# Last image of a convolution-attention layer: which engine takes the outer taps, and where a range check branches

## The chip, the cores and the metric

The kernel runs on one core of a Trainium2 chip. The core has TensorE (PE, with its weight loads shown as PEld), VectorE (DVE), ScalarE (ACT), GpSimd (POOL), and SyncE (SP), which issues most of the DMAs. The metric is the device time of one execution in microseconds. A profile is one execution of the program on the chip, seen by the hardware profiler; its span runs from the first to the last instruction that it recorded.

## The reference

Eight images of 256 channels and 32 x 32 pixels go through two layers. Layer 0 is a convolutional attention block followed by a gated feed-forward block; layer 1 is attention over tokens with a mixture of eight experts. The change touches the feed-forward block of layer 0 and the point where layer 1 begins. Of layer 0, this part counts:

```python
def _edffn(x, pi_w, dw_w, fft_p, po_w):
    x = _conv1x1(x, pi_w)                 # 256 -> 1024 channels
    x = _dwconv3(x, dw_w)                 # 3 x 3 taps, each channel by itself
    x1, x2 = (x[:, :hid], x[:, hid:])
    x = jax.nn.gelu(x1, approximate=False) * x2
    x = _conv1x1(x, po_w)                 # 512 -> 256 channels
    ...
    xf = jnp.fft.rfft2(xp) * fft_p        # on 8 x 8 patches
    xp = jnp.fft.irfft2(xf, s=(PS, PS))
    ...

a = _attention(_ln(x, norm1_w, norm1_b), ...)
x = x + gamma1 * a
f = _edffn(_ln(x, norm2_w, norm2_b), pi_w, dw_w, fft_p, po_w)
return x + gamma2 * f
```

## The kernel before

All of it is float32. A tile has 128 partitions, which hold 128 channels, and in the free dimension the 1024 pixels of an image or half of them (512). The 1024 hidden channels of the feed-forward block are thus eight groups, n = 0 to 7; group n in the first four (x1) is passed through a Gelu and multiplied with group n + 4 (conv).

**Order.** Most instructions are written through a small class (`InOrder`, whose call is line 72, so that nearly every row of the profile has L72). It ties each instruction to the one that was written before it on the same engine. The order on an engine is therefore the order in which the Python generators are stepped: `together(main, side, ratio)` steps `side` as long as its summed costs lag behind those of `main`. Instructions written as `nc.sync`, `nc.vector` and so on are placed by the scheduler.

**A group.** `open_group(b, n, pad)` (L927) makes the 1x1 convolution of one group on PE, half an image at a time (ph, from a pool of two PSUM banks that nearly all of layer 0's small results share). ACT copies each half into a tile with a border of zeros (`pad`: hpad or vpad), and writes the same half, multiplied by the weight of the middle tap, into the group's result. `tap` (L611) then adds one outer tap on DVE: a scalar_tensor_tensor over 128 x 1024 which reads the pad and the result and writes the result. There are eight outer taps, `OTHERS`. `complete` (L1019) follows the last tap: for the last image it issues the Gelu on ACT at once; then `gate` (L1027) multiplies a finished pair on DVE (two halves) and `mix` (L1050) puts the product through the output convolution on PE. `spectrum` (L1065) follows all groups: a copy on ACT (zf), two small transforms on PE (pf, py) with a product on DVE between them (gf), and DVE's sum into the image (t<-py), at whose end the image is stored (td).

**The last image.** For images 0 to 6 the groups run beside the attention of the next image. Image 7 has nothing beside it but the end of image 6's spectrum and the small `scores_matrix` (L1178), which prepares a matrix for layer 1 in a tile called lin; see L1200 to L1204. There `hidden` is given `on_pe=(2,)`: groups 0, 1 and 3 to 7 are convolved on DVE, one opened ahead of the one that runs, and group 2 by `group_on_pe` (L941), which has PE add all nine taps by matmuls with diagonal matrices (taps, pc).

**Range check and branch.** The attention of layer 0 takes exponentials without subtracting a maximum. Their sums and the reciprocals of these are kept in `accs`; after `spectrum(B - 1)` they are compared with a limit, a matmul counts the partitions where all is well (votes), and DVE writes `bad` (L1215). At L1218 every engine loads `bad` from SBUF and branches: only if it is set, `layer0_shifted` computes layer 0 again with a subtracted maximum. What stands inside and behind the branch is scheduled by itself.

**Behind it.** Constants are loaded (vec2, wrs, brs), then from L1365 layer 1 begins: `load_t` (L1374) loads image 0 as layer 0 stored it, `at` and `wv` are weights, and `first_norm(0)` (L1468) transposes image 0 on PE (tpt), copies it on ACT (zt), takes statistics on DVE (st, mv), a root on POOL, scales on DVE and transposes back (tpz). Nothing runs beside this first norm. Its tiles take the SBUF addresses which layer 0's tiles had.

Of the kernel before, what the change touches and what calls it, by code (L numbers as in the profile page):

```python
# [17 lines left out]
P = 128  # L18
# [6 lines left out]
NE = 8  # L25
# [79 lines left out]
def conv_attn_hybrid_kernel(  # L105
# [371 lines left out]
    with ExitStack() as l0:  # L477
# [137 lines left out]
        OTHERS = (0, 1, 2, 3, 5, 6, 7, 8)  # L615

# [324 lines left out]
        def group_on_pe(b, n):  # L941


            assert ready2[b]
            diag = one.tile([P, 9, P], F32, tag="xn", name="taps")
            pad = vpad[n % 2]
            for h in range(2):
                hs = slice(h * HALF, (h + 1) * HALF)
                ph = ps_m.tile([P, HALF], F32, tag="mm", name="ph")
                conv1x1(ph, piw, n * P, xn2[b], hs)  # L950
                act.activation(interior(pad, h), rows(ph), AF.Identity, bias=pi_o[:, n : n + 1])
            for k in range(9):
                act.activation(diag[:, k, :], ident, AF.Copy, scale=dw_w[:, n, k : k + 1])
            yield
            dst = group_tile(n)
            r = H // 2
            for h in range(2):
                pc = ps_m.tile([P, HALF], F32, tag="mm", name="pc")
                for k in range(9):
                    r0 = h * r + k // 3  # L960
                    pe.matmul(pc, diag[:, k, :], inside(pad, r0, k % 3, r), start=(k == 0), stop=(k == 8))
                act.copy(dst[:, h * HALF : (h + 1) * HALF], pc)
                if h == 1:
                    hid_of[b]["h"][n] = dst
                    complete(b)
                yield

        def hidden(b, lead, on_pe=(), alone=False):
# [3 lines left out]
            on_dve = [n for n in range(2 * ng) if n not in on_pe]  # L972
# [19 lines left out]
            hid = hid_of[b] = {"h": {}, "out": [], "gelu": 0, "alone": alone}  # L992
            others = [(g, 3 * i) for i, g in enumerate(on_pe)]
            beside = {}
            for g, at in others:

                beside[at, 6], beside[at + 1, 6], beside[at + 2, 1] = g, g, g
            running = {}
            for m, n in enumerate(on_dve):
                pad, dst = cur  # L1000
                for i, k in enumerate(OTHERS):
                    if m + 1 < len(on_dve):
                        if i == 3:
                            opening = open_group(b, on_dve[m + 1], hpad[(m + 1) % 2])
                            cur = next(opening)
                            next(opening)
                        if i == 5:
                            next(opening)
                    if (m, i) in beside:
                        g = beside[m, i]  # L1010
                        if g not in running:
                            running[g] = group_on_pe(b, g)
                        next(running[g])
                    tap(dst, pad, dw_w[:, n, :], k)
                    yield 1.3
                hid["h"][n] = dst
                complete(b)
# [186 lines left out]
        together(rest(), hidden(B - 1, (), (2,), alone=True), 1.0)  # L1204
# [12 lines left out]

    with tc.If(nc.values_load(bad[0:1, 0:1]) > 0):  # L1218
        layer0_shifted()

    z_d = [dram.tile([P, 2, 3, KC, HALF], F32, tag=f"zd{b}", name=f"zd{b}") for b in range(B)]
    u_d = [dram.tile([P, KC, N], F32, tag=f"ud{b}", name=f"ud{b}") for b in range(B)]
    wm = ctx.enter_context(tc.tile_pool(name="wm", bufs=1))
    more.append(wm.tile([P, NVEC - NVEC0], F32, name="vec2"))  # L1230
    nc.sync.dma_start(more[0], vecs[:, NVEC0:])
    wrs = wm.tile([P, KC, NE], F32, name="wrs")
    nc.sync.dma_start(wrs, wr.rearrange("(k p) e -> p k e", p=P))
    brs = wm.tile([1, NE], F32, name="brs")
    nc.sync.dma_start(brs, br)
    wT = wm.tile([4 * NE, N], F32R, name="wT")
    feats = [wm.tile([P, KC, HALF], F32, name="feat0"), None]
    z2_last = wm.tile([P, KC, HALF], F32, name="z2_last")
    mhalf1 = wm.tile([P, NT], F32, name="mhalf1")
    nc.gpsimd.memset(mhalf1, -0.5)  # L1240

    NG, SLOTS = 2, NE // 2
    w_d = [[dram.tile([P, 3, KC, C], F32, tag=f"wd{e}_{l}", name=f"wd{e}_{l}") for l in range(3)] for e in range(NE)]
    w_in = {}

    def in_parts(e, l):

        return l != 1 or e % 2 == 1

    def load_expert(pool_, e, l):  # L1250

        tag = f"w{e % SLOTS}_{l}"
        if not in_parts(e, l):
            w_ = pool_.tile([P, KC, C], F32, tag=tag, name=tag, bufs=1)
            nc.sync.dma_start(w_, w2[e].rearrange("(k p) o -> p k o", p=P))
        else:
            w_ = pool_.tile([P, 3, KC, C], F32R, tag=tag, name=tag, bufs=1)
            nc.sync.dma_start(w_.bitcast(F32), w_d[e][l])
        w_in[e, l] = w_

    def stacked(dst, src, order):

        first = [order.index(i) for i in range(2)]
        dve.tensor_copy(dst[:, :, first[0]].bitcast(F32R), src)
        dve.tensor_sub(dst[:, :, first[1]].bitcast(F32R), src, dst[:, :, first[0]])
        for i, part in enumerate(order):
            if i not in first:
                dve.tensor_copy(dst[:, :, i], dst[:, :, first[part]])

    def upper(dst, src, eng=None, positive=False):  # L1270

        if eng is None:
            act.activation(dst[:, 0], src, AF.Relu if positive else AF.Copy, scale=DOWN)
        else:
            eng.tensor_scalar_mul(dst[:, 0], src, DOWN)

    def lower_part(dst, src, positive=False):
        high = dst[:, 0].bitcast(F32)
        if positive:
            dve.scalar_tensor_tensor(dst[:, 1], src, 0.0, high, ALU.max, ALU.subtract)  # L1280
        else:
            dve.tensor_sub(dst[:, 1], src, high)

    def difference(dst):
        dve.scalar_tensor_tensor(dst[:, 2], dst[:, 1].bitcast(F32), -STEP, dst[:, 0].bitcast(F32), ALU.mult, ALU.add)

    def layer_norm(src, dst, zt, room, bank):

        n = src.shape[2] // P
        mv = room([P, NT, 2], "mv", 2)  # L1290
        for i0 in range(0, n, 2):
            tp = bank([P, 2, C], "tpt")
            for i in range(2):
                for k in range(KC):
                    c0 = (i0 + i) * P
                    pe.transpose(tp[:, i, k * P : (k + 1) * P], src[:, k, c0 : c0 + P], ident)
            act.copy(zt[:, i0 : i0 + 2, :], tp)
            yield 0.6
            for i in range(i0, i0 + 2):
                st = room([P, 6], "st", 4)  # L1300
                dve.bn_stats(st, zt[:, i, :])
                dve.bn_aggr(mv[:, i, :], st)
            yield 0.6

        y = room([P, NT], "y1", 2)[:, :n]
        r = room([P, NT], "r1", 2)[:, :n]
        pool.tensor_scalar(y, mv[:, :n, 1], LN_EPS, None, ALU.add)
        pool.tensor_tensor(r, y, mhalf1[:, :n], ALU.pow)
        pool.tensor_mul(y, y, r)
        pool.tensor_mul(y, y, r)  # L1310
        pool.tensor_scalar(y, y, -0.5, 1.5, ALU.mult, ALU.add)
        pool.tensor_mul(r, r, y)

        for _ in range(4):
            yield 1.0

        def scaled(i0):
            for i in range(i0, i0 + 2):
                dve.tensor_scalar(zt[:, i, :], zt[:, i, :], mv[:, i, 0:1], r[:, i : i + 1], ALU.subtract, ALU.mult)

        scaled(0)
        yield 1.0
        scaled(2)
        yield 1.0
        for i0 in range(0, n, 2):
            if i0 + 4 < n:
                scaled(i0 + 4)
            tp = bank([P, KC, 2, P], "tpz")
            for i in range(2):
                for k in range(KC):  # L1330
                    pe.transpose(tp[:, k, i, :], zt[:, i0 + i, k * P : (k + 1) * P], ident)
            act.copy(dst[:, :, i0 * P : (i0 + 2) * P], tp.rearrange("p k i c -> p k (i c)"))
            yield 0.9

    def gate(h, room, bank):

        nt = NT // 2
        lg = bank([P, nt, NE], "lg")
        for i in range(nt):
            c0 = i * P  # L1340
# [24 lines left out]
    with ExitStack() as l1:  # L1365
# [45 lines left out]
        def expert_parts():  # L1411

            for e in range(NE):
                for l, src in enumerate((w1, w2, wo)):
                    if not in_parts(e, l):
                        continue
# [230 lines left out]

# [329 lines left out]
```

## Time and profile before

| | us |
|---|---|
| median of 3 runs (lowest, highest) | 3183.1 (3177.9, 3192.1) |
| the profiled execution | 3183.65 |
| its span | 3181.8 |
| busy PE, PEld | 2935.8, 1938.8 |
| busy DVE | 2390.2 |
| busy ACT | 1565.1 |
| busy POOL | 341.0 |
| last image: first tap to last gate | 1322.7 to 1409.3 |
| its spectrum and the check | 1409.3 to 1424.5 |
| from the check to the first matmul of layer 1 | 1424.5 to 1439.4 |
| last instruction that stores the output is issued | 3178.05 |

Busy times are sums over the whole span and say little of a stage of 100 us; what bounds a stretch is read from the stretch alone. In the page's lines "x8" is the number of instructions, and what stands in square brackets is the idle time of the engine before the line and the instruction that ended it. "issue" there means that the profile shows nothing that the engine waited for.

### The profile page before, as it was taken

The page shows a single profiled execution, that of the slowest core. Times are in us where ns is not written, and L with a number is a line of the kernel's source. Part 1 is how long each engine was busy: PE and PEld are TensorE (multiplying, and loading weights), DVE is VectorE, ACT ScalarE, POOL GpSimd, SP SyncE. Part 2 cuts the span into 40 slices and gives each one's busy share as a digit, 9 for nine tenths or more (in the row PEclk, how much of TensorE's full clock was granted, in tenths as well). Part 3 has the DMA queues.
Part 4 walks back from the last instruction along what each step waited for, and adds up shares of the span by engine and source line. Part 5 has one row for each costly group of instructions (what it writes and reads, how often), then busy time and mean ns, then how long its engine had stood idle before and what let it go on. Part 6 is the DMA issues. An engine that isn't in the chain of part 4 may idle for free.

```text
span 3181.8 us, 41598 instructions
## 1 busy us (share of the span) xinstructions
PE 2935.8 (92%) x16802; PEld 1938.8 (61%) x16802; DVE 2390.2 (75%) x3014; ACT 1565.1 (49%) x2312; POOL 341.0 (11%) x419
## 2 busy tenths in 40 slices
PE   5998899899898989868999999999999999999998
PEld 3654555555555555434666666677777777777776
DVE  1378877878787869664767665588988888888887
ACT  1554445555454536313333333365666666666665
POOL 1021211111111110001222222100000000000000
PEclk9998999999999999988999999999999999999999
DMA  5113030212112020002333221422112142211220
GB/s 152 55 27 80 27 80 27 72 36 62 46 47 61 28 66 8 17 14 101 125 131 132 106 103 54 176 76 78 69 67 82 64 172 86 99 67 66 93 73 27
DMA packets 63854, 234.85 MB, mean 74 GB/s; under 512 B 5590, under 2 KB 13862, under 8 KB 54822
## 3 DMA queue, kind: packets, MB, share of 16 engines
q1 hardware_dynamic: 63654, 232.12, 21.9%
q8 instruction: 134, 2.20, 0.3%
q14 instruction: 66, 0.54, 0.1%
HBM read 140.61 MB, written 91.49 MB: 73 GB/s over the span
## 4 chain that ended last, share of the span: by engine, by line
PE 49%; DVE 4%; ACT 1%; issue 0%; POOL 0%; SPq 0%; DMA 0%; ACTq 0%; DVEq 0%
PE pm L72 12%; PE pa L72 11%; PE q L72 11%; PE s L72 4%; PE po L72 4%; PE pv L72 2%; PE pk L72 2%; DVE zt L72 1%; DVE nm L72 1%; PE tp L72 1%; DVE pr L72 1%; PE tpz L72 1%; PE tpt L72 1%; DVE st L72 1%; ACT pr L72 1%
## 5 line engine op out<-in xcount | busy, mean ns | idle before, releaser
L72 PE MATMUL pa<-ze,w 128*128 128x512 f32 x1488 | 423.2, 393 | 0.0
L72 DVE SCALAR_TENSOR_TENSOR x<-hpad,vec,x 128x1024 f32<-128x1024 f32 x248 | 317.0, 1282 | 40.5 <-ACT x L72 33.5
L72 DVE SCALAR_TENSOR_TENSOR conv<-hpad,vec,conv 128x1024 f32<-128x1024 f32 x256 | 329.3, 1293 | 13.9 <-ACT conv L72 7.3
L72 PEld LDWEIGHTS pa<-ze,w 128*128 128x128 f32 x1488 | 278.2, 188 | 63.3 <-issue 3.1
L72 ACT ACTIVATE h<-pa,bn_o,s1a 128x512 f32<-128x512 f32 x256 | 198.7, 776 | 203.4 <-PE pa L72 203.4
L72 ACT ACTIVATE pT<-s 128x1024 f32<-128x1024 f32 x256 | 247.3, 1024 | 71.9 <-PE s L72 71.9
L72 PE MATMUL po<-pT,vT 128*32 128x256 f32 x4096 | 274.0, 385 | 0.0
L72 PE MATMUL q<-h2p,w 128*128 128x512 f32 x768 | 269.0, 459 | 0.0
L72 DVE SCALAR_TENSOR_TENSOR h<-pa,s1b,h 128x512 f32<-128x512 f32 x256 | 191.2, 747 | 93.9 <-PE pa L72 87.8
L72 PE MATMUL ph<-xn,piw 128*128 128x512 f32 x512 | 244.7, 615 | 3.1 <-DVE xn L72 1.6
L72 PE MATMUL pm<-h,w 128*128 128x512 f32 x512 | 240.8, 593 | 0.0
L72 PE MATMUL s<-kk,z 128*128 128x512 f32 x512 | 236.8, 594 | 4.1 <-DVE pr L72 4.1
L72 PE MATMUL q<-z_first,w 128*128 128x512 f32 x768 | 217.2, 391 | 2.7 <-DVE z_first L72 1.7
L72 PE MATMUL pm<-h1p,w 128*128 128x512 f32 x768 | 216.7, 390 | 0.5 <-DVE h1p L72 0.5
L72 DVE SCALAR_TENSOR_TENSOR o<-vpad,pe_w,o 128x1024 f32<-128x1024 f32 x128 | 163.5, 1282 | 45.5 <-ACT o L72 42.3
L72 PEld LDWEIGHTS q<-h2p,w 128*128 128x128 f32 x768 | 144.6, 188 | 83.1 <-issue 59.6
L72 PE MATMUL s<-qst,kst 128*128 128x256 f32 x1024 | 176.1, 314 | 14.5 <-DMA kst<-part 13.2
L72 ACT ACTIVATE hpad<-ph,pi_o 128x512 f32<-128x512 f32 x126 | 86.9, 689 | 182.9 <-PE ph L72 176.0
L72 PEld LDWEIGHTS po<-pT,vT 128*32 128x32 f32 x4096 | 120.8, 110 | 85.9 <-issue 4.2
L72 PEld LDWEIGHTS s<-qst,kst 128*128 128x128 f32 x1024 | 137.5, 193 | 47.8 <-issue 42.9
L72 PEld LDWEIGHTS q<-z_first,w 128*128 128x128 f32 x768 | 144.4, 188 | 34.4 <-DVE z_first L72 2.9
L72 PEld LDWEIGHTS pm<-h1p,w 128*128 128x128 f32 x768 | 144.7, 188 | 31.7 <-DVE h1p L72 0.9
(268 smaller groups left out, 5068.1 us busy)
## 6 DMA issues: line engine op xcount, KB each, us to landing
ze<-zd SPq DMA_DIRECT2D x29, 1536.0 KB, 6.4
qst<-part SPq DMA_DIRECT2D x32, 512.0 KB, 8.7
kst<-part SPq DMA_DIRECT2D x32, 512.0 KB, 14.9
te<-ud SPq DMA_DIRECT2D x32, 512.0 KB, 4.1
wd<-parts_w SPq DMA_DIRECT2D x20, 768.0 KB, 3.7
w<-wd SPq DMA_DIRECT2D x20, 768.0 KB, 4.6
zd<-parts SPq DMA_DIRECT2D x14, 1024.0 KB, 3.8
t<-in_x_dram SPq DMA_DIRECT2D x8, 1024.0 KB, 5.0
```

Of the source, the lines that this page charges most:

```text
L72: return self._tc.keep_in_program_order(method(*args, **kwargs))
```

## The change

It has two parts.

For the last image, `hidden` and `group_on_pe` are replaced by a new function. All eight groups have their taps on DVE, but of group n the first `ON_POOL[n]` outer taps are taken by two other engines: ACT multiplies the shifted image by the tap's weight into a tile (part; four buffers), and POOL adds this to the group's result. Groups are opened two ahead, with four pads (vpad as well as hpad):

```diff
+        ON_POOL = (0, 3, 3, 3, 4, 3, 3, 3)
...
+        def hidden_last(b):
+
+            pads = [hpad[0], hpad[1], vpad[0], vpad[1]]
+            dsts = {}
+            hid = hid_of[b] = {"h": {}, "out": [], "gelu": 0, "alone": True}
+
+            def open_(n):
+                opening = open_group(b, n, pads[n % 4])
+                pad, dsts[n] = next(opening)
+                next(opening)
+                yield 0.0
+                next(opening)
+                for k in OTHERS[: ON_POOL[n]]:
+                    part = two.tile([P, N], F32, tag="pT", name="part", bufs=4)
+                    act.activation(rows(part), inside(pad, k // 3, k % 3, H), AF.Copy, scale=dw_w[:, n, k : k + 1])
+                    pool.tensor_add(dsts[n], dsts[n], part)
+                yield 0.0
+
+            for n in range(2):
+                for _ in open_(n):
+                    pass
+            for n in range(2 * ng):
+                opening = open_(n + 2) if n + 2 < 2 * ng else None
+                for i, k in enumerate(OTHERS[ON_POOL[n] :]):
+                    if opening and i in (0, 2):
+                        next(opening)
+                    tap(dsts[n], pads[n % 4], dw_w[:, n, :], k)
+                    yield 1.3
+                hid["h"][n] = dsts[n]
+                complete(b)
...
-        together(rest(), hidden(B - 1, (), (2,), alone=True), 1.0)
+        together(rest(), hidden_last(B - 1), 1.0)
```

The second part takes the branch from between the layers. All that follows it becomes a function, `tokens`, which is called once without a branch, and a second time inside the branch, at the end of the program, behind `layer0_shifted`. The memory pools of layer 1 are made with `reuse_waits="tile"`, as those of the experts were before, and three of its first loads go to POOL's queue, in order with POOL's other instructions:

```diff
-    with tc.If(nc.values_load(bad[0:1, 0:1]) > 0):
-        layer0_shifted()
...
+    def tokens(stack):
+
+        wm = stack.enter_context(tc.tile_pool(name="wm", bufs=1, reuse_waits="tile"))
...
-        two = l1.enter_context(tc.tile_pool(name="two1", bufs=2))
+            two = l1.enter_context(tc.tile_pool(name="two1", bufs=2, reuse_waits="tile"))
...
-        load_t(0)
+            load_t(0, pool)
             at = wpool.tile([P, KC, C], F32, name="at")
-            nc.sync.dma_start(at, at_d)
+            pool.dma_start(at, at_d)
...
+            wv_s = wpool.tile([P, KC, C], F32, name="wv")
+            pool.dma_start(wv_s, wvT.rearrange("(k p) o -> p k o", p=P))
...
+    with ExitStack() as stack:
+        tokens(stack)
+    with tc.If(nc.values_load(bad[0:1, 0:1]) > 0):
+        layer0_shifted()
+        with ExitStack() as stack:
+            tokens(stack)
```

The rest of the diff is the indentation of what is now inside `tokens`, and the arguments of `hidden` that nothing uses any more.

## Prediction

> **What bounds it now.** I read the page's slices first, then busy time by stretch, then the timelines of DVE and POOL, and last the instructions of the branch. The change lies between 1290 and 1450 us, and at the program's end. The stretches (us, then busy PE, PEld, DVE, ACT, POOL, then TensorE clock and DMA):
>
> ```profile
> 1322.70:1362.10 39.40, 35.89 (x88) 16.26 (x89) 31.36 (x27) 17.86 (x32) 0.00 (x0) 0.96 0.08 34
> 1362.10:1409.30 47.20, 24.52 (x70) 15.46 (x70) 45.99 (x40) 8.80 (x13) 0.00 (x0) 0.81 0.00 0
> 1409.30:1424.50 15.20, 14.08 (x58) 9.71 (x56) 6.28 (x14) 2.24 (x4) 0.00 (x0) 0.82 0.00 1
> 1424.50:1439.40 14.90, 0.00 (x0) 0.02 (x1) 3.02 (x20) 1.79 (x3) 4.62 (x7) 0.64 0.52 182
> ```
>
> In the hidden stage of the last image (1322.7 to 1409.3) DVE sets the end and POOL does nothing; then comes a latency chain, the spectrum, of 15.2 us; then 14.9 us without one matmul, the branch. DVE's timeline in that stage:
>
> ```profile
> 1322.68 1.28 DVE L72 SCALAR_TENSOR_TENSOR x<-hpad,vec,x 128x1024 f32<-128x1024 f32 x1 [4.11 <-ACT x L72]
> 1324.67 30.08 DVE L72 SCALAR_TENSOR_TENSOR x<-hpad,vec,x 128x1024 f32<-128x1024 f32 x23
> 1362.07 10.53 DVE L72 SCALAR_TENSOR_TENSOR conv<-hpad,vec,conv 128x1024 f32<-128x1024 f32 x8 [7.32 <-ACT conv L72]
> 1372.64 1.29 DVE L72 TENSOR_TENSOR hid<-x,conv 128x512 f32<-128x512 f32 x2
> 1373.85 10.52 DVE L72 SCALAR_TENSOR_TENSOR conv<-hpad,vec,conv 128x1024 f32<-128x1024 f32 x8
> ```
>
> Eight taps take 10.52, so a tap costs 1.315 in a row. The 86.6 us are 56 taps (73.6), four gates of 1.21 (4.8), 0.9 for the previous image, and 7.3 idle while PE convolves group 2. Now two places where POOL and DVE read SBUF at once, first in layer 1, then taps beside two POOL copies of half a tile:
>
> ```profile
> 2013.00 2.87 DVE L72 TENSOR_TENSOR parts<-z,parts 128x1024 f32<-128x1024 f32 x1 [1.40 <-ACT parts L72]
> 2012.43 5.64 POOL L72 TENSOR_TENSOR feat<-feat,z 128x1024 f32<-128x1024 f32 x2
> L72 POOL TENSOR_TENSOR feat<-feat,z x12: 2349/2362/3331, 1641.0 to 2014.7; 128x1024 f32<-128x1024 f32 x12
> 791.68 4.38 DVE L72 SCALAR_TENSOR_TENSOR conv<-hpad,vec,conv 128x1024 f32<-128x1024 f32 x3
> 792.30 2.68 POOL L72 COPY vpad<-vfull 128x512 f32<-128x512 f32 x2 [15.95 <-ACT vfull L72]
> ```
>
> The third line gives min/median/max in ns. The DVE operation of 1.22 (a like addition, feat<-feat,scratch, takes 1215 ns) needs 2.87 beside an add and ends only 1.1 us after that add; the second POOL add needs 3.33 instead of 2.35 and ends at 2018.07, 2.20 after DVE's end at 2015.87. They take turns. The boundary and the end:
>
> ```profile
> 1424.40 0.14 DVE L1215 TENSOR_SCALAR bad<-votes 1x1 int32<-1x1 f32 x1
> 1439.41 3.29 PE L72 MATMUL tpt<-ident,t 128*128 128x128 f32 x16 [15.48 <-DMA at<-at_d]
> 1441.27 0.43 DVE L72 BATCH_NORM_STATS2 st<-zt 128x6 f32<-128x256 f32 x1 [2.84 <-ACT zt L72]
> L1218 SPq COMPARE_BRANCH  x1: 50/50/50, 1425.5 to 1425.5; - x1
> L1218 SPq EVENT_SEMAPHORE  x8: 17/17/17, 1426.0 to 1430.1; - x8
> L1218 DVEq COMPARE_BRANCH  x1: 72/72/72, 1425.2 to 1425.2; - x1
> L1218 DVEq EVENT_SEMAPHORE  x1: 21/21/21, 1431.5 to 1431.5; - x1
> 3178.05 0.37 SPq L1808 DMA_DIRECT2D out_dram<-te  x1
> ```
>
> DVE resumes 6.2 us after its branch, ACT and POOL likewise; SP, which jumps over few instructions, after 0.4. Then the loads of layer 1 are issued, and the first statistics come at 1441.27, 16.8 us after the last t<-py (1424.48).
>
> [...]
>
> **The change, part by part.** *Taps.* ON_POOL sums to 22, so DVE keeps 64-22 = 42 taps: 42 x 1.315 = 55.2, with gates 4.8 and the 0.9. PE's group (18 matmuls, nine ACT taps) and DVE's 7.3 idle go. ACT gets 22 products of about 1.05 (as x<-x) and one more opening: some 7 us per group against DVE's 12 to 13, so it keeps ahead; four pads and four part buffers let it. POOL gets 22 adds of 128x1024. *Price of an add on DVE:* one tap and one add in turn take 2.20 + 1.1 + 0.07 (a tap is that much longer than the 1.22) = 3.35, less the tap's 1.315: 2.03. From below, a half-size, one-input copy cost the taps 0.23 (4.38 against 3.92, for two); four times the reads make 0.92. From above, the whole 2.35. I take 2.03: 22 x 2.03 = 44.7 (20 to 52). Nothing hides it: all adds come while DVE has taps queued. *Opening two ahead:* the first step of the generator now opens groups 0, 1 and half of 2 before tap 0. PE's last py of image 6 then stands behind ph of groups 1 and 2, each half waiting for a PSUM bank that ACT frees (1.46 per half): py at about 1326.5 instead of 1321.1, and t<-py is behind tap 0 on DVE, in order, with all further taps behind it: idle 1324.0 to 1327.2, +3.2. Sum 55.2+4.8+0.9+44.7+3.2 = 108.8 against 86.6: **+22.2**.
>
> *Branch gone from the boundary.* t(0), at and wv go to POOL's queue, which is in order behind the adds; by tile sizes t(0) falls on lin, free after about 1335, so it lands long before layer 0 ends. The first transposes then follow the last py on PE, zt's copy takes 0.59, and the first statistics come some 1.3 after the last t<-py, not 16.8: **-15.5**. If the loads wait, bound 8 to 10. What is late next is the chain of the first norm itself (1441.3 to 1449.4), unchanged. The small work that lay in the gap (DVE 3.0, ACT's table load 1.8, POOL's 4.6) loses its cover; the spectrum's idle DVE time can take it, 0 to 4, I take **+1**.
>
> *Branch at the end.* SP is last: store issued until 3178.43, load of bad 0.5, branch 0.1, and now it jumps over the whole second copy of layer 1 as well, so I give it the far target's 6.2, then 0.6 of semaphores, 0.6 of final waits and 0.8 of barrier: 3187.2 instead of 3181.8, as the store's landing (3180.9) is covered. **+5.5** (3 if SP's target comes quickly, 7 at most).
>
> Sum: 22.2 - 15.5 + 1 + 5.5 = +13.2 on the profiled execution's 3183.65 (span 3181.8 and 1.85 around it), which is 0.5 above the median of 3183.1: **3197**. A difference under 0.5% (15.9 us) can't be told from none with this kernel.
>
> **Rivals.** (1) The adds hide beside the taps. For it: POOL is empty, and ACT and PE have room. Against: the 2.87. At no cost for adds the stage is 64.1, -22.5, in all -31.5: 3152. At the lower price, 0.92, it is -11: 3172. (2) The slower side: the boundary still holds layer 1's loads until layer 0's last tiles are free, or the POOL queue issues t(0) only then. From a landing later than the last t<-py it costs; with 5.2 us from issue to landing (1434.07 to 1439.27) the first statistics come 7 after, the gain is 9.8, and the time 3203. For it: one POOL queue, adds first. Against: the addresses, and that the last group's adds are issued two groups early. (3) The branch isn't dear at the end: 3 instead of 5.5 gives 3194; it only shifts the forecast.
>
> **Numbers.** Forecast with (3) 0.67, own range 3187 to 3207, of which about two thirds lie below 3199; rival (2) 0.17; rival (1) 0.16. Faster 0.15 (nearly all of (1)), same 0.46, slower 0.39. The range, 3175 to 3211, takes in the cheaper adds and the dearer ones, and leaves out most of (1).
>
> **What would show it.** Right: POOL busy some 60 us between 1322 and 1432, its adds at 3.3 instead of 2.35, taps beside them spaced 3.3; the last gate near 1431; tpt within 1 us of the last py; SP's last semaphores near the end of the span 6 us after its branch. Wrong: taps at 1.3 beside running adds, DVE waiting for part, a gap before tpt, or ACT ending the waits of the taps.

## The result, and the profile after

The changed kernel takes 3192.7 us (median of 15 runs, 3188.5 to 3196.3) where the kernel before takes 3182.9 (15 runs): a ratio of 1.0029, with a 95% interval of 1.0021 to 1.0037. It is slower by about 10 us, 0.3%. The profiled execution has a span of 3191.4 us against 3181.8.

Cut at the same events in both traces, the span splits so (us, each from the start of the instruction named):

| stretch | before | after | difference |
|---|---|---|---|
| span's start to the last image's first tap | 1322.68 | 1323.08 | +0.4 |
| first tap to the end of the last gate | 86.62 | 108.72 | **+22.1** |
| last gate to the end of the last t<-py (spectrum) | 15.18 | 14.02 | -1.2 |
| last t<-py to layer 1's first statistic (boundary) | 16.79 | 1.92 | **-14.9** |
| first statistic to the issue of the last store | 1736.78 | 1737.41 | +0.6 |
| that issue to the span's end | 3.75 | 6.27 | **+2.5** |
| span | 3181.80 | 3191.42 | +9.6 |

Busy time by stretch of the changed kernel, in the columns used before (us, busy PE, PEld, DVE, ACT, POOL, clock, DMA share, GB/s): first half and second half of the hidden stage, spectrum, and what was the gap at the branch.

```profile
1323.10:1362.70 39.60, 22.75 (x58) 10.63 (x58) 35.84 (x17) 25.16 (x32) 27.53 (x9) 0.80 0.10 36
1362.70:1431.80 69.10, 27.62 (x70) 16.44 (x69) 68.11 (x36) 21.43 (x26) 48.78 (x23) 0.67 0.06 23
1431.80:1445.82 14.02, 12.92 (x57) 8.90 (x56) 6.25 (x14) 4.04 (x7) 1.03 (x1) 0.88 0.00 0
1445.82:1449.00 3.18, 1.94 (x16) 1.73 (x16) 3.08 (x25) 2.05 (x4) 0.00 (x0) 1.00 0.84 273
```

POOL, idle there before, is now busy for 76.3 us of the two halves, and DVE is busy for 103.95 of 108.7 us though it has fourteen taps fewer. A DVE instruction counts as busy also while something holds it up: the twelve taps in the third row below fill 28.73 us, 2.39 each, where a tap in a row takes 1.315. The rows below show DVE's taps and POOL's adds, each from its own timeline (start, duration in us, and in brackets the idle time ahead).

```profile
1323.08 1.28 DVE L72 SCALAR_TENSOR_TENSOR x<-hpad,vec,x 128x1024 f32<-128x1024 f32 x1 [4.11 <-ACT x L72]
1327.73 0.87 DVE L72 SCALAR_TENSOR_TENSOR t<-py,vec,t 128x256 f32<-128x256 f32 x2 [3.37 <-PE py L72]
1328.53 28.73 DVE L72 SCALAR_TENSOR_TENSOR x<-hpad,vec,x 128x1024 f32<-128x1024 f32 x12
...
1444.05 1.77 DVE L72 SCALAR_TENSOR_TENSOR t<-py,vec,t 128x256 f32<-128x256 f32 x4 [0.64 <-PE py L72]
...
1447.74 0.42 DVE L72 BATCH_NORM_STATS2 st<-zt 128x6 f32<-128x256 f32 x1
```

```profile
1327.60 18.80 POOL L72 TENSOR_TENSOR x<-x,part 128x1024 f32<-128x1024 f32 x6 [21.34 <-ACT part L72]
...
1422.34 0.81 POOL L72 DMA_DIRECT2D t<-td  x1 [0.27 <-issue]
...
1425.47 3.92 POOL L1387 TENSOR_SCALAR_AFFINE_SELECT sel<-sel 32x1024 f32<-32x1024 f32 x2
```

From 1327.60 on, POOL runs six adds without a pause, 18.80 us or 3.13 each; DVE's twelve taps in 28.73 include stretches with and without an add beside them. There is no bracket on the DVE row: nothing made it wait by a semaphore. The time is inside the instructions. The view of the adds as a group, by tile, with min/median/max in ns:

```profile
L72 POOL TENSOR_TENSOR conv<-conv,part x13: 2673/3203/3433, 1362.7 to 1418.1; 128x1024 f32<-128x1024 f32 x13
...
L72 POOL TENSOR_TENSOR x<-x,part x9: 2360/3210/3322, 1327.6 to 1359.5; 128x1024 f32<-128x1024 f32 x9
```

The add that starts at 1327.60, while DVE is idle, takes 2.36. The median is 3.2: beside taps an add is stretched as well, by some 0.85 us. At the boundary PE has the first transpose 0.1 us after the last t<-py (1445.82), and the loads that had been behind the branch were issued by POOL's queue at 1422.34 already (t<-td, 5.9 us to landing), ahead of the spectrum:

```profile
1445.92 1.94 PE L72 MATMUL tpt<-ident,t 128*128 128x128 f32 x16 [0.66 <-DVE bad L1208]
```

At the end of the program, the branch (instructions of line 1849 in the tile view's columns: duration min/median/max in ns, first and last start):

```profile
L1849 SPq EVENT_SEMAPHORE  x8: 17/17/17, 3189.3 to 3189.8; - x8
...
L1849 POOLq COMPARE_BRANCH  x1: 45/45/45, 2130.5 to 2130.5; - x1
...
L1849 PEldq COMPARE_BRANCH  x1: 3835/3835/3835, 3182.2 to 3182.2; - x1
...
L1849 SPq COMPARE_BRANCH  x1: 50/50/50, 3186.1 to 3186.1; - x1
```

SP resumes 3.1 us after its branch (3186.1 + 0.05 to 3189.3). In the kernel before, where only the second computation of layer 0 stands inside the branch, it needed 0.4. But the others, which needed 5.7 to 6.3 there, now take 2.8 to 3.8. POOL, which has no work after 2130, branches at 2130.5 already.

### The profile page after: what moved, and what is told of

Read it like the earlier page. It is cut to its first block, busy times and chain, and to the rows that moved or that the text cites. A ratio compares the mean times of both kernels' runs of the same rounds, so it can differ in the third digit from the quotient of the medians.

```text
span 3191.4 us, 41548 instructions
## 1 busy us (share of the span) xinstructions
PE 2922.1 (92%) x16766; PEld 1931.6 (61%) x16766; DVE 2415.3 (76%) x3000; ACT 1585.3 (50%) x2325; POOL 416.5 (13%) x444
## 4 chain that ended last, share of the span: by engine, by line
PE 76%; DVE 15%; ACT 3%; POOL 2%; DMA 2%; issue 2%; SPq 0%; ACTq 0%; DVEq 0%; POOLq 0%
PE pm L72 12%; PE pa L72 11%; PE q L72 11%; PE po L72 10%; PE s L72 8%; PE ph L72 6%; DVE conv L72 3%; DVE x L72 3%; PE pq L72 3%; PE sums L72 3%; DVE o L72 2%; PE pz L72 2%; PE pv L72 2%; PE pk L72 2%; DVE hid L72 1%
## 5 line engine op out<-in xcount | busy, mean ns | idle before, releaser
L72 DVE SCALAR_TENSOR_TENSOR conv<-hpad,vec,conv 128x1024 f32<-128x1024 f32 x233 | 303.8, 1311 | 5.8
L72 PE MATMUL ph<-xn,piw 128*128 128x512 f32 x512 | 251.3, 628 | 28.5 <-ACT conv L72 12.9
L72 PEld LDWEIGHTS ph<-xn,piw 128*128 128x128 f32 x512 | 94.4, 198 | 139.9 <-issue 95.4
L72 PE MATMUL pz<-pow__116,hid 128*128 128x256 f32 x512 | 136.1, 421 | 34.6 <-DVE hid L72 34.6
## 6 DMA issues: line engine op xcount, KB each, us to landing
kst<-part SPq DMA_DIRECT2D x32, 512.0 KB, 14.9
```

Of the source, the lines that this page charges most:

```text
L72: return self._tc.keep_in_program_order(method(*args, **kwargs))
```

## The experiments

All times are medians; each ratio is against runs of the kernel before on the same chip in the same session. "Stage" is first tap to last gate, "boundary" and "end" are cut as in the table above.

| kernel | us | ratio, 95% interval | stage | boundary | end |
|---|---|---|---|---|---|
| branch alone moved | 3169.9 | 0.9971 (0.9961, 0.9981) | 88.3 | 1.9 | 6.6 |
| taps alone moved | 3201.1 | 1.0059 (1.0046, 1.0072) | 107.2 | 16.7 | 3.7 |
| no taps for POOL | 3176.9 | 0.9986 (0.9978, 0.9995) | 94.5 | 1.9 | 6.7 |
| add of part to itself | 3180.1 | 0.9994 (0.9985, 1.0002) | 98.8 | 1.9 | 6.4 |
| add of another tile | 3193.8 | 1.0032 (1.0021, 1.0042) | 108.9 | 1.9 | 6.4 |
| fill instead of add | 3150.5 | 0.9896 (0.9881, 0.9911) | 65.5 | 1.9 | 6.3 |
| copy instead of add | 3163.7 | 0.9937 (0.9922, 0.9952) | 80.7 | 1.9 | 6.7 |
| no branch at all | 3188.3 | 1.0017 (1.0010, 1.0024) | 108.8 | 1.9 | 3.9 |
| transfer at the branch | 3191.4 | 1.0023 (1.0014, 1.0031) | 108.7 | 1.9 | 6.5 |
| last image stored early | 3183.1 | 0.9997 (0.9989, 1.0006) | 86.6 | 14.4 | 3.7 |
| two ahead, one group on PE | 3163.3 | 0.9943 (0.9929, 0.9956) | 81.0 | 1.9 | 6.8 |
| two ahead, two groups on PE | 3158.9 | 0.9919 (0.9905, 0.9932) | 73.0 | 1.9 | 7.0 |

### The two parts by themselves

The changed kernel with the hidden stage of before, and the kernel before with the new hidden stage:

```diff
 # branch alone moved: in the changed kernel
-        together(rest(), hidden_last(B - 1), 1.0)
+        together(rest(), hidden(B - 1, (), (2,), alone=True), 1.0)
 # taps alone moved: in the kernel before
-        together(rest(), hidden(B - 1, (), (2,), alone=True), 1.0)
+        together(rest(), hidden_last(B - 1), 1.0)
```

> Only the second part: layer 1 follows without a branch, the branch stands at the program's end, and image 7 is convolved as before (group 2 on PE, no POOL adds). Theory (the lock: POOL's adds and DVE's taps exclude each other, and the parts simply add up): the two traces give -14.9 us at the boundary, +2.5 at the end and about -0.5 between, so about 3170, with the last gate of layer 0 where it was before (1409). Rival (the boundary gained only because the new stage left PE, ACT or the SP queue early): well under 10 us gained, 3174 or more.

> Only the first part: the taps of image 7 by ACT and POOL, groups two ahead, none on PE; the branch stays between the layers. Lock theory: the hidden stage is 22 us longer, so about 3205, and the sum of this and of the branch-only kernel is the whole change. Rival (the stage is long because layer 1's early loads and constants are mixed into it): less than 15 us longer, under 3198.

Measured: 3169.9 and 3201.1, that is -12 and +19 us by the medians; the ratios say -9 (between -12 and -6) and +19 (between +15 and +23). Together this is +7 to +10, which agrees with the +10 of the whole change. So the change is a gain of 9 to 12 from the branch and a larger loss from the taps, and the stretches lie where the table above has them (boundary 1.92, stage 107.2). The stage with the taps alone grew by 20.6, where 22 was expected, and the kernel came to 3201 and not 3205. With the branch alone the stage is 1.7 longer than before: POOL's constants for layer 1, which used to be made in the gap, now run beside the taps (a gate of 2.20 us instead of 1.29, a row of eight taps of 11.35 instead of 10.52). With the taps alone moved they are still made in the gap, and the stage is 1.5 shorter than in the changed kernel.

### Is it POOL's part, or the new order of the groups?

```diff
-        ON_POOL = (0, 3, 3, 3, 4, 3, 3, 3)
+        ON_POOL = (0, 0, 0, 0, 0, 0, 0, 0)
```

> The changed kernel with ON_POOL all zero: every outer tap on DVE, POOL adds nothing, groups still opened two ahead and none on PE. Lock theory: 64 taps of 1.315 make 84.2, with gates 4.8, 0.9 and the wait of 3.4 93 us in place of the 108.7 with POOL's help, so about 15 us faster than the changed kernel: 3177. Rival (adds cost DVE little, the stage is long for its order or for ACT): 22 more taps of 1.315, 29 us slower: 3221.

All 64 outer taps on DVE, and 3176.9: 16 us faster than with POOL's help, 14.2 of them in the stage itself. So it is POOL's part. A tap given to ACT and POOL costs DVE more than a tap kept: 14.2 / 22 = 0.65 us more.

### What is the price of an add: waiting for its result, or the memory?

Four kernels leave everything in place and change what POOL does with the partial product. In all four no tap and no gate uses what POOL computes, and 22 of the last image's 64 outer taps are left out of the result.

```diff
-                    pool.tensor_add(dsts[n], dsts[n], part)
+                    pool.tensor_add(part, part, part)               # add of part to itself
+                    pool.tensor_add(part, part, xn2[b][:, 0, :])    # add of another tile
+                    pool.memset(part, 0.0)                          # fill
+                    pool.tensor_copy(part, part)                    # copy
```

> The changed kernel, but POOL adds each part to itself and not to the group's result, so that no tap waits for an add: 22 of the 64 outer taps are left out of the result. Same engines, same shapes, two SBUF inputs. Lock theory: within 2 us of the changed kernel, 3191 to 3195, taps beside an add still 3.3 us apart. Rival (DVE waits for POOL's results at the start of each group): the stage shrinks to 64 to 70 us, about 3150.

Measured: 3180.1, which fits neither. The rival (the taps waited for POOL's results) is far off at 3150, but the cost was a quarter less than the theory had it. The trace showed why the experiment was not clean: an add of a tile to itself is a shorter instruction, 1.89 us where it runs alone. So it was repeated with two different tiles, and with instructions that read one tile and none:

> The 22 adds of POOL now add another tile of the same size to the partial product and leave the sum in the partial product; nobody waits for it, and 22 of the last image's 64 outer taps are left out of the result. An add of two different tiles should take 2.36 us where it runs alone, as in the changed kernel. If what an add costs VectorE is the time in which it holds it from the memory (2.03 us each in the changed kernel), the stage stays at 107 to 109 us and the kernel at 3191 to 3195. If the cost was that taps or gates waited for the adds to arrive, the wait is gone here and the stage is 42 x 1.315 + 6 + 3 = 64 us: 3150 (no more than 3155). 3180, what adding a tile to itself gave, would mean that its shorter duration was not the reason for that result.

> POOL's 22 adds are replaced by 22 copies of the partial product onto itself (one input; 22 of the last image's 64 outer taps are left out of the result). If the price of a POOL instruction to VectorE is its own duration less 0.3 us whatever it reads, a copy of about 0.9 to 1.0 us costs 0.6 to 0.7 each and the stage is 77 to 80 us: 3162 to 3165. If only instructions with two inputs hold VectorE off, the stage is 64 to 66 us: 3147 to 3151.

> POOL's 22 adds are replaced by 22 fills of the same tile with zero (no input is read; 22 of the last image's 64 outer taps are left out of the result). If only POOL's reads of two tiles hold VectorE off, the taps keep 1.31 us each, the stage is 64 to 66 us and the kernel 3147 to 3151. If every POOL instruction on a tile of this size alternates with the taps, by its own duration less 0.3 us, a fill of 0.5 to 1 us costs 0.2 to 0.7 each: 3152 to 3163.

All three times came out where the theory puts them in which POOL's reads hold DVE off: 3193.8, 3163.7 and 3150.5. (The copies' stage, 80.7, is just above the 77 to 80 that were expected.) POOL's rows in the four traces, by tile, in the order in which they stand in the table:

```profile
L72 POOL TENSOR_TENSOR part<-part x22: 1892/2868/2874, 1324.7 to 1406.9; 128x1024 f32<-128x1024 f32 x22
```

```profile
L72 POOL TENSOR_TENSOR part<-part,xn x22: 2352/3316/3344, 1328.9 to 1418.2; 128x1024 f32<-128x1024 f32 x22
```

```profile
L72 POOL MEMSET part<- x22: 951/952/956, 1325.6 to 1374.7; 128x1024 f32 x22
```

```profile
L72 POOL COPY part<-part x22: 1036/2002/2087, 1326.8 to 1390.4; 128x1024 f32<-128x1024 f32 x22
```

The first number is the shortest, an instruction by itself; the second, the median, is one beside taps. Everything that reads grows by 0.96 to 0.98 us; the fill doesn't grow at all. DVE's side, from its timeline of the fill and of the add of another tile:

```profile
1326.52 15.68 DVE L72 SCALAR_TENSOR_TENSOR x<-hpad,vec,x 128x1024 f32<-128x1024 f32 x12
...
1377.24 8.06 DVE L72 SCALAR_TENSOR_TENSOR conv<-vpad,vec,conv 128x1024 f32<-128x1024 f32 x5
```

```profile
1329.80 15.68 DVE L72 SCALAR_TENSOR_TENSOR x<-hpad,vec,x 128x1024 f32<-128x1024 f32 x5
```

In the same 15.68 us DVE gets through twelve taps where POOL fills for some 6 us of the time (1.31 each), and through five where POOL adds without a pause (3.14 each). The five taps in 8.06 stand beside POOL's affine selects of layer 1 (2 x 1.5 us), which read SBUF: 1.5 us more than five taps alone (6.56).

With the fill as the base, since it has the same constants in its stage and no hold-up by the 22 instructions, the price of one POOL instruction to DVE is the stage's growth over 22:

| POOL's instruction | alone, us | stage | price to DVE, us |
|---|---|---|---|
| fill | 0.95 | 65.55 | 0 (the base) |
| copy, one input | 1.04 | 80.66 | (80.66 - 65.55) / 22 = 0.69 |
| add of one tile to itself | 1.89 | 98.82 | 1.51 |
| add of two tiles | 2.35 | 108.88 | 1.97 |
| the changed kernel's adds | 2.36 | 108.72 | 1.96 |

In each row with reads the price is the instruction's own duration less 0.35 to 0.40. The changed kernel's adds, for whose results gates and taps must wait, cost no more than adds whose results nobody uses (the two stages differ by 0.2 us), so a wait for results is no part of the cost. DVE's shorter instructions pay it too: the two halves of a gate, 1.29 us by themselves, took 5.46 beside adds in the changed kernel, some 2.1 more for each half.

```profile
1395.44 5.46 DVE L72 TENSOR_TENSOR hid<-x,conv 128x512 f32<-128x512 f32 x2
```

### The branch

```diff
 # no branch at all: in the changed kernel, the shifted recomputation left out with it
-    with tc.If(nc.values_load(bad[0:1, 0:1]) > 0):
-        layer0_shifted()
-        with ExitStack() as stack:
-            tokens(stack)
```

> The changed kernel with the range check's branch and what stands behind it (the shifted recomputation) left out: no branch at the end at all. The end, from the last output's issue to the span's end, should go back from 6.3 to 3.7 us (its length in the kernel before): 2.5 us off the changed kernel's 3193, so 3190 to 3191. Were the branch at the end worth the 5.5 us that the prediction gave it, 3187 to 3188.

The end is 3.9 us instead of 6.3, and the time 3188.3, 3.1 below the kernel with a further transfer, measured in the same session (below; in effect the changed kernel), and 4.4 below the changed kernel's own median from another session. The trace's 2.4 is the direct reading; the time lies between the two that were expected and does not separate them by itself.

Why did the branch take 5.7 to 6.3 us in the middle of the kernel before, and about 3 at the end? When the engines branched there, the last image's 1 MB store (td<-t, issued at 1424.5) was in flight. Two kernels were to test this:

```diff
 # transfer at the branch: in the changed kernel
+    nc.sync.dma_start(t_d[0], t_d[1])
     with tc.If(nc.values_load(bad[0:1, 0:1]) > 0):
 # last image stored early: in the kernel before, in spectrum() and ahead of the last hidden stage
-            nc.sync.dma_start(t_d[b], t[b])
+            if b < B - 1:
+                nc.sync.dma_start(t_d[b], t[b])
...
+        nc.sync.dma_start(t_d[B - 1], t[B - 1])
         together(rest(), hidden(B - 1, (), (2,), alone=True), 1.0)
```

> The changed kernel with one more transfer, 1 MB within the chip's DRAM (it overwrites a scratch image that nobody reads again), issued by SP just ahead of the branch at the end. If an engine at the branch waits for its instructions' fetch, and the fetch queues behind transfers on the same DMA engines, SP takes 5 us or more from its branch to its next semaphore, as in the kernel before where a store of 1 MB was in flight, instead of 3.1. If the place in the program and not the transfer made the difference, it stays at 3.1 us, though the end of the span may come later by the transfer itself.

This kernel does not test it: the statement is placed by the scheduler, and the transfer was issued at 1449.8, in the first norm of layer 1. The end was 6.5 us, much as without it (6.3).

> The kernel before, in which the last image's t is stored before its depthwise stage instead of after its spectrum, so that no transfer is in flight at the branch in the middle; the last image's second residual addition is left out of what layer 1 reads. If the 5.7 to 6.2 us that the branch took there was the fetch behind the 1 MB store, PE goes from its branch to its semaphore in 3 to 4 us, and the stretch from the last image's last residual addition to layer 1's first statistic falls from 16.8 to 13.5 to 14.5: 3179 to 3181. If not, 5.7 us remain and the stretch stays at 16 or more: 3182 to 3183.

The branch in the trace of that kernel, and below it the same row of the kernel with the store in its old place:

```profile
L1220 PEldq COMPARE_BRANCH  x1: 3807/3807/3807, 1425.3 to 1425.3; - x1
...
L1220 DVEq COMPARE_BRANCH  x1: 72/72/72, 1425.3 to 1425.3; - x1
...
L1220 DVEq EVENT_SEMAPHORE  x1: 21/21/21, 1429.3 to 1429.3; - x1
```

```profile
L1218 PEldq COMPARE_BRANCH  x1: 5687/5687/5687, 1425.2 to 1425.2; - x1
```

Without the store in flight PE's branch takes 3.81 instead of 5.69, which is what it takes at the end of the changed kernel (3.84); DVE resumes after 3.9 instead of 6.2; and the boundary falls from 16.8 to 14.4. So in the trace some 2 us of the branch in the middle came with the store.

The DMA view shows what the store did. The profile lists the packets that bring instructions as queues of their own (columns: packets, MB, share of the 16 DMA engines). In the kernel before only the store (queue q1) moves from 1425 to 1428, and the instructions follow between 1428.0 and 1428.5:

```profile
q1 hardware_dynamic: 138, 1.04, 87.3%
...
q14 instruction: 4, 0.03, 15.4%
q8 instruction: 1, 0.02, 11.3%
```

With the store early, five such packets move between 1426 and 1427:

```profile
q14 instruction: 4, 0.03, 11.9%
q8 instruction: 1, 0.02, 8.6%
```

In both kernels PE, ACT, POOL and DVE resume 2 to 3.5 us after these packets. So the packets of instructions came behind the store, and the engines resumed behind these packets; that the branch waits for them is read from this order alone. Two more things stay open. SP's own semaphores at the branch run until 1430.1 in the kernel before, about when the store had landed, and until 1426.3 with the store early; no run separates this wait from that for the instructions. And a transfer in flight need not cost as much: at the end of the changed kernel SP branches at 3186.1, just as the packets of the last output (512 KB) begin to move, and still resumes after 3.1 us, as DVE does after 3.0.

The expected 3179 to 3181 did not appear: the time is 3183.1, and against the kernel before the interval goes from -3.5 to +1.9 us. In the profiled execution the stretch of layer 1 is 2.3 longer (1739.1), but that stretch varies from 1736.8 to 1740.8 over all the traces here, so whether the 2.4 us survive to the end is open.

### A version that beats both

If adds are dear and the branch's place is worth 9 to 12 us, what is left to take is DVE's wait for a group that has just been opened. In the kernel with the branch alone moved it stands in DVE's timeline:

```profile
1359.04 10.53 DVE L72 SCALAR_TENSOR_TENSOR conv<-hpad,vec,conv 128x1024 f32<-128x1024 f32 x8 [7.29 <-ACT conv L72]
```

The new function without POOL, with group 2 on PE as before, and with only group 0 opened ahead of the first tap:

```diff
+            pads = [hpad[0], hpad[1], vpad[1]]
+            groups = [0, 1, 3, 4, 5, 6, 7]
...
+            aside = group_on_pe(b, 2)
+            plan = {(0, 1): 1, (0, 3): 1, (0, 5): 2, (0, 7): 2}
...
+                    if (m, i) in plan:
+                        half(plan[m, i])
+                    if m >= 1 and i in (0, 2):
+                        half(m + 2)
+                    if (m, i) in ((1, 4), (1, 6), (2, 4)):
+                        next(aside)
+                    tap(dst, pad, dw_w[:, n, :], k)
```

> No partial products on POOL; group 2 of the last image on PE as in the kernel before; the seven others on VectorE, opened two ahead in three pads, only the first before its first tap; range check's branch at the end. Against the kernel with the branch alone moved (3170, stage 88.3 us), VectorE's waits for a group that has only just been opened (7.3 us the largest, 9.2 in all) should go: stage 56 x 1.315 + 4.8 + 0.9 + 1 to 2 = 80 to 82 us, and the kernel at 3162 to 3165. If group 2's matmuls or ACT's nine scaled weight tiles come in the way of the openings instead, a wait of the same size returns at another group and it stays at 3168 to 3172.

3163.3, and a stage of 80.96, as expected. DVE's rows have neither the wait of 7.3 nor the 3.4 at the head:

```profile
1316.66 1.29 DVE L72 SCALAR_TENSOR_TENSOR x<-hpad,vec,x 128x1024 f32<-128x1024 f32 x1 [4.11 <-ACT x L72]
1317.87 0.87 DVE L72 SCALAR_TENSOR_TENSOR t<-py,vec,t 128x256 f32<-128x256 f32 x2
1318.65 19.64 DVE L72 SCALAR_TENSOR_TENSOR x<-hpad,vec,x 128x1024 f32<-128x1024 f32 x15
1338.21 10.53 DVE L72 SCALAR_TENSOR_TENSOR x<-vpad,vec,x 128x1024 f32<-128x1024 f32 x8
1348.65 10.52 DVE L72 SCALAR_TENSOR_TENSOR conv<-hpad,vec,conv 128x1024 f32<-128x1024 f32 x8
```

Then group 5 on PE too:

```diff
-            groups = [0, 1, 3, 4, 5, 6, 7]
+            groups = [0, 1, 3, 4, 6, 7]
...
-            aside = group_on_pe(b, 2)
+            aside = (group_on_pe(b, 2), group_on_pe(b, 5))
+            at = {(1, 2): 0, (1, 4): 0, (1, 6): 0, (2, 5): 0, (3, 3): 1, (3, 5): 1, (3, 7): 1, (5, 5): 1}
...
```

> Built on the kernel with two groups open ahead (3163, stage 80.96 us): group 5 of the last image goes to PE as well, beside group 2, and its place in VectorE's order is taken by group 6. VectorE gives up eight taps of 1.315 us: stage 70 to 72 us and the kernel 3152 to 3155, if PE, which was busy for 10.3 of 15 and 8.6 of 15 us in the stretches from 1360 on, takes the 16 us of matmuls without holding a gate or an opening. If the gates' matmuls or ACT's scaled weight tiles now stand in the way, a wait of 4 us or more shows on VectorE before a gate, and the kernel stays at 3158 to 3163.

3158.9, and a stage of 73.0: eight us of it are gone, where nine to eleven were expected. The time lies at the lower edge of the rival's 3158 to 3163, and what the rival names is there, if shorter than its 4 us: DVE waits 2.8 us for a gate, because the copy of PE's second group is done only at 1387.3 (idle ahead of the row, in brackets):

```profile
1377.98 6.55 DVE L72 SCALAR_TENSOR_TENSOR conv<-vpad,vec,conv 128x1024 f32<-128x1024 f32 x5
1387.36 2.62 DVE L72 TENSOR_TENSOR hid<-x,conv 128x512 f32<-128x512 f32 x4 [2.82 <-ACT conv L72]
```

It is 23 us (0.8%) faster than the kernel before and, across sessions, 34 faster than the changed one, the best found here.

## Why the prediction was right, point by point

The forecast was 3197, called a difference too small to tell; it is 3193, and 15 runs of each kernel do tell the 0.3% from none (interval 0.21% to 0.37%). The sum was +13.2, the traces give +9.6.

- **The taps' price: right.** Estimated at 2.03 us an add from one case in layer 1 where DVE and POOL take turns (2.87 us for a DVE addition of 1.22), measured at 1.96; the stage was put at 108.8 and is 108.72. What made it right: an add was priced by the time for which it holds DVE off, not by the DVE instructions that it saves. Some of the closeness is luck. Of the 108.72, 1.5 are POOL's constants for layer 1, which the forecast had elsewhere; with the taps alone moved the stage is 107.2. The terms of the price, 2.20 + 1.1 + 0.07, add up to 3.37 and not 3.35; and a tap beside adds without a pause comes every 3.14 us, not every 3.3. The rival that adds hide beside taps would have been 3152; the kernel with fills shows that world, 3150.5. The lower bound, 0.92, was scaled up by reads from half-size copies; a whole copy costs 0.69, and an add with twice its reads 1.97. POOL's adds last 70 us in all (22 x 3.2); the "some 60" among the signs was too low, and did not follow from the 3.3 an add beside it.
- **The head of the stage: right.** 3.37 idle ahead of t<-py, 3.2 estimated, ended by PE's py. The kernel with one group opened ahead of the first tap has none of it.
- **The boundary: right.** -14.9 where -15.5 was put. The first statistics come 1.92 after the last t<-py instead of 1.3, since nineteen small instructions for layer 1's constants stand ahead of them on DVE. The rival in which the loads still wait at the boundary falls: t(0) was issued at 1422.34 and landed by 1428.3, 17 us ahead of the transposes.
- **The small work of the gap: about the right size, in other places.** +1 was put. POOL's selects cost the taps 1.5 us inside the stage, DVE's constants cost 0.6 at the boundary (in the 1.92 above), and the spectrum became 1.2 shorter, which was not foreseen. Its cause was not tried: it is 12.3 to 15.2 us long over the traces.
- **The branch at the end: the mis-sized term.** +5.5 was put (its terms add up to 5.4), with 6.2 us from SP's branch to its target; 3.1 were measured, and the end is +2.5. This is rival (3), which had 3 and 3194. That SP, with more to jump over, would need DVE's 6.2 instead of its own 0.4 was the author's estimate from the trace of before; no run varies the length of a jump by itself. The compare-and-branch itself took 45 to 76 ns on SP, DVE, ACT and POOL at the end; they resumed 2.8 to 3.1 us after it. The error was to carry over a duration from a place in which a 1 MB store was in flight; in the kernel that stores early DVE resumes 3.9 us after the same branch instead of 6.2, and the instructions move 2 us sooner. The rest, from 3.9 to 3.1, is not explained.

## What to carry to other kernels

Moving elementwise work from DVE to an idle POOL lost time here. Beside DVE's taps, which read two tiles, each of POOL's adds and copies cost DVE its own duration less 0.35 to 0.40 us (an add 1.96, a copy 0.69), and a fill cost nothing; a tap that was moved saved 1.315. Set this price against the DVE time saved before work is moved. DVE instructions that read one tile were not tried. A gap in which every engine waits, like a branch between two stages, can go almost whole once the loads behind it can go ahead: here 14.9 of 16.8 us went, and 2.5 came back at the branch's new place. DVE's wait for a group just opened, 7.3 us, went with opening two ahead, without POOL. Take the price of an event from a place with the same traffic beside it: PE's branch took 5.69 us with a 1 MB store in flight and 3.81 without.

## What the runs showed of the hardware that was not expected

- An add of a tile to itself is shorter than an add of two tiles on POOL: 1.89 against 2.35 us for 128x1024 float32.
- POOL's fill of 0.95 us beside two-input DVE instructions costs these nothing (1.31 a tap), and a copy of nearly the same length (1.04) costs 0.69.
- The same branch took PE 5.69 us with a 1 MB store in flight and 3.81 without it; the packets of instructions moved at 1428.0 behind the store, and at 1426.0 without it. POOL, with its instruction stream at an end 1050 us before the others, took 2.8.
